# Regrouped sums, early first steps of two layers, and a moved verdict in a four-layer graph network

## The chip, the core and the metric

The kernel runs on one core of one Trainium2 chip. The metric is the device time of one execution in microseconds, as the median of several runs. A core has a matrix engine (TensorE, PE in the profile; PEld is its loading of weights), VectorE (DVE), ScalarE (ACT), GpSimd (POOL) and SyncE (SP), which here only issues DMAs. Each engine takes its instructions in order. DMAs are issued by SP, ACT or POOL, and stand in that engine's queue like any other instruction.

## The reference

A graph network of four layers on x, 2708 nodes of 512 float32 features, with a dense 0/1 adjacency matrix adj (2708 x 2708, int32, symmetric, some 2.3% ones). Every layer normalizes, cuts at zero, and adds its result to x:

```python
h = jnp.maximum(_layernorm(x, axis=-1), 0.0)
x = x + layer(h, adj)
```

The layers, cut to what matters:

```python
# layer 0
out = (a.T @ X) @ weight
out = relu(out * norm[:, None])            # norm = clip(in_degree, 1) ** -0.5
# layer 1: only the first 64 neighbours of a row count
keep = Ab & (jnp.cumsum(Ab, axis=1) <= 64)
xj = leaky_relu((keep @ X / cnt) @ W_nb.T + b_nb)
xi = leaky_relu(X @ W_line.T + b_line)
out = xi + xj
# layer 2: graph attention, 8 heads of 64
Wh = einsum('nd,hdo->hno', x, W)           # f1, f2 = Wh . a1, Wh . a2
e = leaky_relu(f1[:, :, None] + f2[:, None, :], 0.2)
attention = softmax(where(adj > 0, e, NEG_INF))
out = elu(attention @ Wh)
# layer 3
self_f = x @ W_self + b_self
nb_f = (mask @ x / deg) @ W_nb + b_nb
out = relu(concat([self_f, nb_f]) @ W_comb + b_comb)
```

## The kernel before

**Tiling.** The nodes lie in NC = 22 chunks of R = 126 rows; the last chunk has 62. Helper `move` (lines 88 to 99) is one DMA for a full chunk (line 99) and two for the last, 48 and 14 rows (lines 96, 97). A layer first has a dense part, with its product by the weights, and then sums over neighbours. A float32 product is kept as two parts (`halves`), so that a sum costs two matmuls per pair of chunks, one for the last chunk, whose two parts share a tile. PSUM has eight buffers (`ps`), each holding one accumulator, product or set of transposes.

**Sums.** The 22 chunks of results are worked in groups of 4, 4, 4, 4, 3, 3 (line 102): for each group the loop runs over all 22 chunks m, so that a unit (group, m) makes one weight tile of up to 504 columns from the stored pattern vT, and multiplies it with the halves of chunk m into the group's accumulators. For layers 1 and 3 this is `aggregate` (lines 339 to 367). The weight tile is made two units ahead in three buffers; at m = 11 `before` issues the loads for the group's results; the accumulators of a group are taken over by `after` in the first units of the next group, one chunk per unit, and those of the last group after the last unit. For layer 1 the weight tile is a comparison and product on VectorE (`weight1`, L594), and `after1` makes two VectorE operations (L607, L610), an add on GpSimd (L613) and a store. For layer 3 it is a cast on VectorE (`weight3`, L1161), and `after3` is two VectorE operations (L1170, L1173) and a store of the output on ACT's queue.

**Layer 0's sums** have a list of their own with staged delays (lines 399 to 528): adjacency block loaded (`load0`), counted (`count0`), its sign taken (`sign0`), multiplied (`multiply0`), which also transposes the pattern into vT. At the end of a group, `multiply0` scales by the degree, with relu on ACT (L505) or VectorE (L496) by turns, and adds to x on GpSimd (L508).

**Dense parts.** `dense` gives four stages, `load`, `normalize` (`norm`: statistics L188, L190, a square root on ACT L192, then hn at L200 or L202), `transpose` (`relu_T`, four transposes L211 and a relu to hT L213) and `multiply`. `staged` runs stage k of chunk c at step c + k. x tiles have five buffers; hn, y and the output share three buffers by their tag "t". Further stages are appended to the list: for layer 1 `save_last` and `spread_last`; for layer 2 `save_last2`, `sums2` (dot products f1 and f2, L783, L785) at lag 4 and `rows2` at lag 5, which turns a chunk's f1 into a row (`row2`, L796) and starts, in its last four chunks, the attention's first steps (`make`, L724).

**Start and end.** In the preamble (lines 272 to 312) each of two weights is turned (16 transposes at L287, four copies on ACT L288), then multiplied by W_comb (`fused`, L293). In the end a verdict is worked out ahead of layer 3's sums (lines 1133 to 1157): short reductions over the degrees, f12 and the largest weights say whether the fast way holds; a matmul sums them over partitions (L1150). All engines read it behind the kernel, to decide whether a general way has to run, which doesn't happen with this input.

Kernel time therefore runs: preamble, layer 0's dense part and sums, layer 1's dense part and sums, layer 2's dense part, attention, layer 3's dense part, layer 3's sums. The order of the instructions on each engine is that of the program, apart from small movements by the scheduler.

Of the kernel before, what the change touches and what calls it, by code (L numbers as in the profile page):

```python
# [44 lines left out]
def fast_layers(  # L45
# [58 lines left out]
    groups = [list(range(sum(sizes[:g]), sum(sizes[: g + 1]))) for g in range(len(sizes))]  # L104
    KMAX = max(sizes)
# [110 lines left out]
    def staged(count, *stages):  # L216

        for step in range(count + max(lag for lag, _ in stages)):
            for lag, fn in stages:
                if 0 <= step - lag < count:  # L220
                    fn(step - lag)
# [50 lines left out]
    with tc.tile_pool(name="pre", bufs=2) as pre:  # L272
# [9 lines left out]
        for i in range(2):  # L282
            wsT = pre.tile([P, NF, D], F32, name="wsT")
            for f in range(NF):
                pt = ps.tile([P, NF, P], F32, name="wsT_ps", tag="ps")
                for k in range(NF):
                    nc.tensor.transpose(pt[:, k, :], ws[i][:, f, k * P : (k + 1) * P], ident)  # L287
                nc.scalar.copy(wsT[:, :, f * P : (f + 1) * P], pt)  # L288
            wf = pre.tile([P, NF, D], F32, name="wf")
            for f in range(NF):  # L290
                po = ps.tile([P, D], F32, name="fused_ps", tag="ps")
                for k in range(NF):
                    nc.tensor.matmul(  # L293
                        po,
                        wsT[:, k, f * P : (f + 1) * P],
                        wc[:, i * NF + k, :],
                        start=(k == 0),
                        stop=(k == NF - 1),
                    )
                nc.vector.tensor_copy(wf[:, f, :], po)  # L300
            nc.gpsimd.dma_start(fused[i].rearrange("(k p) o -> p k o", p=P), wf)
# [37 lines left out]
    def aggregate(weight_of, parts, before, after, lead=2):  # L339

        units = [(g, m) for g in range(len(groups)) for m in range(NC)]
        weight, loaded, acc = {}, {}, {}

        def make(i):
            g, m = units[i]
            weight[i] = weight_of(m, groups[g])

        def multiply(i):  # L350
            g, m = units[i]
            cs = groups[g]
            if m == 0:
                for c in cs:
                    acc[c] = ps.tile([P, D], F32, name="acc", tag="ps")
            for k, c in enumerate(cs):
                matmuls(acc[c], parts[m], weight[i], k, m)
            del weight[i]
            if m == NC // 2:
                loaded.update((c, before(c)) for c in cs)  # L360
            if g and m < len(groups[g - 1]):
                c = groups[g - 1][m]
                after(c, acc.pop(c), loaded.pop(c))

        staged(len(units), (0, make), (lead, multiply))
        for c in groups[-1]:
            after(c, acc.pop(c), loaded.pop(c))
# [7 lines left out]
    with ExitStack() as ring_ctx:  # L375
        ring = ring_ctx.enter_context(tc.tile_pool(name="ring", bufs=NC - 1, side="right"))

# [16 lines left out]
        with tc.tile_pool(name="l0", bufs=2) as wk:  # L394
# [59 lines left out]
            def multiply0(i):  # L454
# [29 lines left out]
                nc.scalar.copy(vT[g][:, :, m * R : (m + 1) * R], pt[:R, :K, :R])  # L484
                if m == NC // 2:
                    xs.update((c, load_x(x_in, c)) for c in cs)
# [4 lines left out]
                for k, c in enumerate(cs):  # L491
                    n = rows(c)
                    xc = xs.pop(c)
                    r = common.tile([P, D], F32, name="y", tag="t", bufs=3)
                    if k % 2:
                        nc.vector.tensor_scalar(  # L496
                            r[:n],
                            acc.pop(c)[:n],
                            0.0,
                            nrm[:n, k : k + 1],  # L500
                            op0=ALU.max,
                            op1=ALU.mult,
                        )
                    else:
                        nc.scalar.activation(  # L505
                            r[:n], acc.pop(c)[:n], AF.Relu, scale=nrm[:n, k : k + 1]
                        )
                    nc.gpsimd.tensor_tensor(xc[:n], xc[:n], r[:n], ALU.add)  # L508
                    sums1[c] = xc
# [76 lines left out]
        staged(NC, *dense(x1, product1), (3, save_last), (4, spread_last))  # L586
# [17 lines left out]
        def after1(c, acc, xc):  # L604
# [8 lines left out]
            nc.gpsimd.tensor_tensor(xc[:n], xc[:n], y[:n], ALU.add)  # L613
            sums1[c] = xc
            if c not in groups[-1]:
                save2(c)
# [12 lines left out]
        aggregate(weight1, h1, before1, after1)  # L629
# [176 lines left out]
    LATE = NC - 4  # L806

    def rows2(c):
# [5 lines left out]
        if c == NC - 4:  # L814
# [4 lines left out]
        if c > NC - 4:  # L819
# [3 lines left out]
    def save_last2(c):  # L823
        if c < len(groups[-1]):
            save2(groups[-1][c])

    more = [(3, save_last2), (4, sums2), (5, rows2)]
    staged(NC, *dense(x2, product2, False, more, scalar=True))
# [252 lines left out]
    with ExitStack() as stack:  # L1081
# [49 lines left out]


        bad = const.tile([P, 7], F32, name="bad")
        with tc.issue_after(final):
            nc.vector.tensor_reduce(bad[:, 0:1], ind, AX.X, ALU.add)
        nc.vector.tensor_reduce(bad[:, 1:2], deg, AX.X, ALU.add)
        nc.vector.tensor_tensor(bad[:, 0:1], bad[:, 0:1], bad[:, 1:2], ALU.subtract)
        nc.vector.tensor_reduce(bad[:, 2:3], deg, AX.X, ALU.min)
        nc.vector.tensor_scalar(bad[:, 2:3], bad[:, 2:3], 0.5, None, op0=ALU.is_lt)
        for i, (op, over, sign) in enumerate(((ALU.max, ALU.is_gt, 1), (ALU.min, ALU.is_lt, -1))):  # L1140
            f = bad[:, 3 + i : 4 + i]
            with tc.issue_after(final):
                nc.vector.tensor_reduce(f, f12.rearrange("p c h -> p (c h)"), AX.X, op)
            nc.vector.tensor_scalar(f, f, sign * F_MAX, None, op0=over)
            nc.vector.tensor_scalar(
                bad[:, 5 + i : 6 + i], wmax[:, i : i + 1], sign * W_MAX, None, op0=over
            )
        nc.vector.tensor_reduce(bad[:, 1:2], bad[:, 2:], AX.X, ALU.max)
        pv = ps.tile([P, 2], F32, name="verdict_ps", tag="ps")
        nc.tensor.matmul(pv[:1], ones, bad[:, 0:2], start=True, stop=True)  # L1150

        differ = small.tile([1, 2], F32, name="differ")
        nc.vector.tensor_scalar(
            differ[:, 0:1], pv[:1, 0:1], float(N - P * NC), None, op0=ALU.not_equal
        )
        nc.vector.tensor_copy(differ[:, 1:2], pv[:1, 1:2])
        nc.vector.tensor_tensor(verdict, differ[:, 0:1], differ[:, 1:2], ALU.add)

# [4 lines left out]

        def before3(c):
            return load_x(x3, c), load_x(s3, c, name="sc", pool=wk, bufs=4)

        def after3(c, acc, loaded):
# [8 lines left out]
            move(nc.scalar, out[c * R : c * R + n, :], xc[:n])  # L1176
# [630 lines left out]
```

## Time and profile before

| | us |
|---|---|
| median of 3 runs | 1862.52 (1861.09 to 1865.51) |
| profiled execution | 1866.35 |
| its span, first to last instruction | 1864.5 |
| mean granted TensorE clock | 0.991 of full speed |

Times within the profile are counted from the span's start. The span in 40 equal slices, each digit the busy share of a slice in tenths, shows how the stages follow:

```profile
PE   8999999989999999989999999999999899999997
PEld 4555776654446887744444344444344455478886
DVE  4655888875444566577889999999999777533333
ACT  2545887862120000046597766776743566400000
POOL 0000111121110112056200000000000222100000
PEclk9999999999999999999999999999999999999999
```

A slice is 46.6 us. Layer 0's sums end at 405 us, layer 1's dense part and sums follow and end at 795.7 (the first of its weight tiles are made far ahead, at 431.1), layer 2's dense part runs to about 900, attention to 1450, layer 3's dense part to 1633 and its sums to 1855. The weight tiles of layers 1 and 3 in the list of groups (busy us, mean ns of one, idle of the engine before them):

```profile
L594 DVE SCALAR_TENSOR_TENSOR kt<-lastr,index,vT 126x504 fp32r<-126x504 int16 (+1 forms) x132 | 105.0, 804 | 82.8 <-PE acc L331 82.8
L1161 DVE CAST kt<-vT 126x504 fp32r<-126x504 int8 (+1 forms) x132 | 52.8, 400 | 141.6 <-PE acc L331 141.5
```

There are 6 groups times 22 units, 132, in both layers. The accumulating matmul is line 331; one takes 0.2325 us when nothing disturbs it.

### The profile page before, as it was taken

To read this page: it belongs to the slowest core of one execution; us is meant where nothing else is said; L and a number is where in the kernel's file an instruction comes from. 1 tells how busy PE (TensorE), PEld (TensorE's weight loads), DVE (VectorE), ACT (ScalarE), POOL (GpSimd) and SP (SyncE) were. 2 spreads that over 40 slices of the span, in tenths; PEclk is the share of its full clock that TensorE was granted. 3 is DMA by queue.
4 is the path that set the end of the run, shared out by engine and by line. 5 is a ranking of instruction groups with operands and counts; after the bars stand their busy time and mean duration, and the time that the engine had idled before them with its cause. 6 is when DMAs were issued, how large, how long until landed. Compare 5 with 4: busy or idle time off the path is not lost.

```text
span 1864.5 us, 30673 instructions
## 1 busy us (share of the span) xinstructions
PE 1808.8 (97%) x11878; PEld 1053.9 (57%) x11878; DVE 1315.9 (71%) x1949; ACT 843.1 (45%) x1536; POOL 214.6 (12%) x194
## 2 busy tenths in 40 slices
PE   8999999989999999989999999999999899999997
PEld 4555776654446887744444344444344455478886
DVE  4655888875444566577889999999999777533333
ACT  2545887862120000046597766776743566400000
POOL 0000111121110112056200000000000222100000
PEclk9999999999999999999999999999999999999999
DMA  6423555542223112243321220221112444303221
GB/s 209 136 79 95 159 156 155 148 127 63 71 73 82 45 45 68 63 142 106 104 73 37 58 54 15 58 60 40 28 33 51 119 134 136 100 22 106 93 67 44
DMA packets 126039, 161.03 MB, mean 86 GB/s; under 512 B 57406, under 2 KB 77994, under 8 KB 125002
## 3 DMA queue, kind: packets, MB, share of 16 engines
q1 hardware_dynamic: 106764, 123.51, 23.1%
q10 hardware_dynamic: 18544, 33.37, 5.5%
q0 software_dynamic: 576, 2.10, 0.4%
q8 instruction: 95, 1.56, 0.3%
q14 instruction: 60, 0.49, 0.1%
HBM read 111.34 MB, written 47.42 MB: 85 GB/s over the span
## 4 chain that ended last, share of the span: by engine, by line
PE 62%; DVE 16%; issue 5%; DMA 4%; ACT 2%; POOL 1%; DVEq 0%; SPq 0%; ACTq 0%; POOLq 0%
PE acc L331 27%; DVE t L724 10%; PE av L908 8%; PE nb_ps L183 8%; PE line_ps L183 4%; PE sums L908 4%; PE self_ps L183 4%; PE wh_ps L183 3%; DVE cum L429 3%; DMA rb<-rT 2%; PE hT_ps L211 1%; DMA x<-x 1%; DMA ai<-in_adj 1%; PE vT_ps L472 1%; ACT cum L444 1%
## 5 line engine op out<-in xcount | busy, mean ns | idle before, releaser
L724 DVE SCALAR_TENSOR_TENSOR t<-rb,ec,vT 126x2708 f32<-126x2708 f32 (+2 forms) x220 | 532.4, 2470 | 16.7 <-PE sums L908 9.8
L908 PE MATMUL av<-t,whs 126*32 126x451 f32 (+3 forms) x4576 | 434.7, 513 | 0.6 <-DVE ln_mv L190 0.6
L331 PE MATMUL acc<-halves,kt 126*126 126x512 f32 x1848 | 431.1, 394 | 0.5 <-DVE kt L594 0.5
L331 PEld LDWEIGHTS acc<-halves,kt 126*126 126x126 f32 x1848 | 343.7, 186 | 85.5 <-DVE kt L594 1.9
L908 PEld LDWEIGHTS av<-t,whs 126*32 126x32 f32 (+1 forms) x4576 | 161.7, 110 | 203.8 <-issue 179.8
L331 PE MATMUL acc<-halves,ar 126*126 126x512 f32 x924 | 254.7, 415 | 5.2 <-ACT vT L484 4.6
L742 ACT ACTIVATE b<-t,eb 126x2708 bf16<-126x2708 f32 (+1 forms) x78 | 199.0, 2551 | 22.1 <-DVE t L724 22.0
L331 PEld LDWEIGHTS acc<-halves,ar 126*126 126x126 f32 x924 | 164.7, 188 | 49.9 <-issue 9.2
L594 DVE SCALAR_TENSOR_TENSOR kt<-lastr,index,vT 126x504 fp32r<-126x504 int16 (+1 forms) x132 | 105.0, 804 | 82.8 <-PE acc L331 82.8
L1161 DVE CAST kt<-vT 126x504 fp32r<-126x504 int8 (+1 forms) x132 | 52.8, 400 | 141.6 <-PE acc L331 141.5
L429 DVE TENSOR_TENSOR_SCAN cum<-ai,deg 126x504 int16<-126x504 int32 (+2 forms) x110 | 126.1, 1157 | 34.5 <-DMA ai<-in_adj 20.3
L192 ACT ACTIVATE ln_rs<-ln_mv,eps 126x1 f32<-126x1 f32 x88 | 25.4, 293 | 276.5 <-DVE ln_mv L190 270.4
L908 PE MATMUL sums<-t,whs 126*32 126x338 f32 (+5 forms) x1568 | 139.1, 448 | 6.0 <-ACT out L947 5.8
L713 ACT ACTIVATE whs<-wh,ef 126x64 f32<-126x64 f32 x220 | 76.3, 349 | 126.6 <-PE sums L908 72.8
L875 POOL TENSOR_SCALAR z<-y 126x512 f32<-126x512 f32 x22 | 44.0, 2000 | 662.5 <-DVE y L868 653.8
L444 ACT ACTIVATE cum<-cum,limit 126x504 int16<-126x504 int16 (+3 forms) x132 | 88.4, 670 | 64.3 <-DVE deg L437 62.3
L188 DVE BATCH_NORM_STATS2 ln_st<-x 126x6 f32<-126x512 f32 x88 | 60.4, 687 | 56.5 <-DMA x<-x 46.4
L908 PEld LDWEIGHTS sums<-t,whs 126*32 126x32 f32 (+1 forms) x1568 | 55.3, 109 | 73.6 <-issue 37.7
L183 PE MATMUL nb_ps<-wfn,hT 128*126 128x512 f32 x176 | 80.9, 603 | 3.1 <-ACT hT L213 3.1
L183 PE MATMUL wh_ps<-w2s,hT 128*126 128x512 f32 (+1 forms) x176 | 82.8, 615 | 0.0
L484 ACT CAST vT<-vT_ps 126x504 int8<-126x504 f32 (+1 forms) x132 | 69.9, 535 | 26.6 <-DVE sums L475 17.1
L183 PE MATMUL h_ps<-w0s,hT 128*126 128x512 f32 x176 | 80.1, 598 | 1.3 <-ACT hT L213 1.3
(174 smaller groups left out, 1981.8 us busy)
## 6 DMA issues: line engine op xcount, KB each, us to landing
x<-x SPq DMA_DIRECT2D x105, 252.0 KB
x<-x ACTq DMA_DIRECT2D x84, 252.0 KB
ai<-in_adj SPq DMA_DIRECT2D x84, 249.0 KB
x<-in_x SPq DMA_DIRECT2D x42, 252.0 KB
rb<-rT SPq DMA_DIRECT2D x7, 1332.8 KB
wh<-whd SPq DMA_DIRECT2D x70, 94.5 KB
whd<-wh SPq DMA_DIRECT2D x21, 252.0 KB
aT<-avT SPq DMA_DIRECT2D x21, 252.0 KB
```

The costliest lines, as they stand in the source:

```text
L183: nc.tensor.matmul(po[:n], lhsT[:, f, :n], w[:, f, :], start=(f == 0), stop=(f == NF - 1))
L188: nc.vector.bn_stats(st[:n], xc[:n])
L331: nc.tensor.matmul(acc[:R], weight[:, k * R : (k + 1) * R], parts[:, i, :], start=(m == 0 and i == 0), stop=(m == NC - 1),)
L429: nc.vector.tensor_tensor_scan(cum[:n, :gw], ai[:n, :gw], ai[:n, :gw], 0.0 if g == 0 else deg[:n, m : m + 1], op0=ALU.add, op1=ALU.max,)
L444: nc.scalar.activation(cum[:n, :gw], cum[:n, :gw], AF.Sign, bias=limit[:n], scale=-1.0, accum_out=signs[:n, m, g : g + 1],)
L484: nc.scalar.copy(vT[g][:, :, m * R : (m + 1) * R], pt[:R, :K, :R])
L594: nc.vector.scalar_tensor_tensor(by_chunk(kt, cs), lastr[:, cs[0] * R : (cs[-1] + 1) * R].rearrange("p (c r) -> p c r", r=R), index[:R, m ...
L713: nc.scalar.activation(t[:q, :O], wh.pop((u, m))[:q], AF.Copy, scale=by)
L724: ins = nc.vector.scalar_tensor_tensor(t[:q, : hi - lo], row[h][:q, lo:hi], ec[:q, m, h : h + 1], vT[g][:q, k, lo:hi], op0=ALU.max, op1=AL ...
L742: nc.scalar.activation(b[:q, : hi - lo], weight[s][:q, : hi - lo], AF.Sigmoid, bias=eb[:q, m, h : h + 1], scale=STEEP,)
L908: nc.tensor.matmul(p[j * S : (j + 1) * S, : b - a], lhsT, rhs[:, part * size + a : part * size + b], start=(s % NC == 0), stop=(s % NC == ...
L1161: nc.vector.tensor_copy(by_chunk(kt, cs), pattern(m, cs))
```

## The change

It has seven parts.

1. In the preamble both weights get their tiles at the front. The second weight's transposes and copies are put between the first weight's product rows 1 and 2.
2. `aggregate` (layers 1 and 3) uses `spans` of 4, 4, 4, 4, 3, 2, 1 chunks; layer 0's sums and the pattern keep the groups. A seventh span adds 22 units and 22 weight tiles to each of the two layers; there are as many matmuls as before.
3. The first three steps of the dense part of layer 1 are issued at m = 9, 13 and 18 of layer 0's last group, those of layer 2 at the same places of layer 1's last span; `staged` goes on from step 3 (`done`).
4. In layer 0's last group the relu stays in PSUM, and the add to x runs on VectorE. In layer 1's last span the add runs on VectorE too.
5. `rows2` comes one step later (lag 6), and the attention's first steps begin at chunk NC - 5 in place of NC - 4, so at the same step as before.
6. The verdict is a function `judge`, called from `before3` in the middle of layer 3's third span.
7. The last chunk's output goes out as 16 rows on ACT's queue and 46 on SP's, in place of 48 and 14 on ACT's.

```diff
+    cuts = [0, 4, 8, 12, 16, 19, 21, NC]
+    spans = [list(range(a, b)) for a, b in zip(cuts, cuts[1:])]
...
-    def staged(count, *stages):
+    def staged(count, *stages, done=0):
-        for step in range(count + max(lag for lag, _ in stages)):
-            for lag, fn in stages:
-                if 0 <= step - lag < count:
-                    fn(step - lag)
+        for step in range(done, count + max(lag for lag, _ in stages)):
+            emit_step(step, count, stages)
+
+    def emit_step(step, count, stages):
+        for lag, fn in stages:
+            if 0 <= step - lag < count:
+                fn(step - lag)
...
+        turn_weight(0)
+        for f in range(NF):
+            if f == NF // 2:
+                turn_weight(1)
+            fuse(0, f)
+        for f in range(NF):
+            fuse(1, f)
...
-    def aggregate(weight_of, parts, before, after, lead=2):
+    def aggregate(weight_of, parts, before, after, lead=2, ahead=()):
...
-        units = [(g, m) for g in range(len(groups)) for m in range(NC)]
+        units = [(g, m) for g in range(len(spans)) for m in range(NC)]
...
             if m == NC // 2:
                 loaded.update((c, before(c)) for c in cs)
+            if g == len(spans) - 1:
+                for at_m, fn, *args in ahead:
+                    if m == at_m:
+                        fn(*args)
...
+        AHEAD = (9, 13, 18)
+        stages1 = dense(
+            x1,
+            lambda *args: product1(*args),
+            more=[(3, lambda c: save_last(c)), (4, lambda c: spread_last(c))],
+        )
...
+                if g == len(groups) - 1 and m in AHEAD:
+                    emit_step(AHEAD.index(m), NC, stages1)
...
+                    po = acc.pop(c)
+
+                    r = po
+                    if g < len(groups) - 1:
+                        r = common.tile([P, D], F32, name="y", tag="t", bufs=3)
...
-                    nc.gpsimd.tensor_tensor(xc[:n], xc[:n], r[:n], ALU.add)
+                    eng = nc.gpsimd if g < len(groups) - 1 else nc.vector
+                    eng.tensor_tensor(xc[:n], xc[:n], r[:n], ALU.add)
...
-        staged(NC, *dense(x1, product1), (3, save_last), (4, spread_last))
+        staged(NC, *stages1, done=len(AHEAD))
...
-            nc.gpsimd.tensor_tensor(xc[:n], xc[:n], y[:n], ALU.add)
+            eng = nc.vector if c in spans[-1] else nc.gpsimd
+            eng.tensor_tensor(xc[:n], xc[:n], y[:n], ALU.add)
             sums1[c] = xc
-            if c not in groups[-1]:
+            if c not in spans[-1]:
                 save2(c)
...
+        stages2 = dense(
+            x2,
+            lambda *args: product2(*args),
+            False,
+            [(3, lambda c: save_last2(c)), (4, lambda c: sums2(c)), (6, lambda c: rows2(c))],
+            scalar=True,
+        )
+        ahead = [(m, emit_step, step, NC, stages2) for step, m in enumerate(AHEAD)]
+        aggregate(weight1, h1, before1, after1, ahead=ahead)
...
-    LATE = NC - 4
+    LATE = NC - 5
...
-        if c == NC - 4:
+        if c == LATE:
...
-        if c > NC - 4:
+        if LATE < c <= LATE + 3:
...
+        def judge():
...
         def before3(c):
+            if c == 2 * KMAX:
+                with tc.issue_after(final):
+                    judge()
...
-            move(nc.scalar, out[c * R : c * R + n, :], xc[:n])
+            half = n // 32 * 16 if c == NC - 1 else n
+            nc.scalar.dma_start(out[c * R : c * R + half, :], xc[:half])
+            if half < n:
+                nc.sync.dma_start(out[c * R + half : c * R + n, :], xc[half:n])
```

The body of `judge` is the verdict of before, word for word, but for the `issue_after` marks, which now stand around the call. The bodies of `turn_weight` and `fuse` are the two inner loops of the preamble, and the DMA of a fused weight is issued behind its fourth row.

## The prediction

> **What bounds the kernel now.** I read the engine totals first, then the list of what the matrix engine waited for, then the timeline and the granted clock around each of those waits. The totals:
>
> ```profile
> PE 1808.8 (97%) x11878; PEld 1053.9 (57%) x11878; DVE 1315.9 (71%) x1949; ACT 843.1 (45%) x1536; POOL 214.6 (12%) x194
> ```
>
> TensorE (PE) is busy for 1808.8 of 1864.5 us, so all but 55.7 us of the span is matrix work, and the change leaves the number of matmuls as it is. It can only win inside those 55.7 us, and in the stretches where PE runs at a lowered clock behind a gap. Who causes the gaps (engine, line waited for, us in total, times, longest):
>
> ```profile
> PE hT_ps L211 <- DVE hn L202: 6.4, 3, 4.2
> ...
> PE hT_ps L211 <- ACT hn L200: 5.3, 2, 4.3
> ...
> PE fused_ps L293 <- ACT wsT L288: 3.2, 2, 2.5
> ...
> PE f_ps L796 <- DVE f L785: 3.0, 2, 2.7
> PE verdict_ps L1150 <- DVE bad L1148: 2.7, 1, 2.7
> ```
>
> Each of these five is touched by the change. The PE timeline shows where they lie, and what follows a gap (start, length, then in brackets the idle time before):
>
> ```profile
> 409.49 1.07 PE L211 MATMUL hT_ps<-ident,hn 126*128 126x126 f32 x4 [4.20 <-DVE hn L202]
> 410.90 1.07 PE L211 MATMUL hT_ps<-ident,hn 126*128 126x126 f32 x4 [0.33 <-DVE hn L202]
> 411.77 5.16 PE L183 MATMUL nb_ps<-wn,hT 128*126 128x512 f32 x8
> 416.76 3.60 PE L183 MATMUL line_ps<-wl,hT 128*126 128x512 f32 x8
> ```
>
> Four transposes cost 0.6 us and eight products 3.60 at full clock. After the gap they take 1.07 and 5.16: the granted clock was 0.51 from 408 to 412 and 0.64 from 412 to 416. A gap thus costs its idle time and a slow stretch behind it.
>
> **The change part by part.** Sums are made against the profiled execution, 1866.35 us (span 1864.5); the median of the runs, 1862.52, lies 3.8 below it, and I take the same gain off that.
>
> *1. Preamble.* PE waits 2.50 at 28.38 because the four copies of the second turned weight (27.77 to 29.79 on ACT) stand behind a table load and square roots from 24.43 on. In the new order these transposes and copies come between the second and third of the first weight's four product rows, at about 16, before that table load. The second weight's loads were issued from 8.13 to 10.47, so they have landed. The first weight's last two product rows (3.9 us each, 15.7 for four) cover the copies (4 x 0.5). Gain **2.5** (0 if the copies still fall behind the roots).
>
> *2. Layer 0 to layer 1.* The last sum ends at 405.3; before, PE next transposes the third normalized chunk at 420.19. After, the first chunk's transposes lie among the last sums; the second chunk's run at 405.5, its neighbour follows: products 406.1 to 409.5 and 409.5 to 413.0. Then the third chunk is late. Its x1 load needs the buffer of chunk 19, whose way out still begins at the same place: two relus of 0.62 from 405.82, an add (now VectorE's instead of GpSimd's), the second chunk's transposed relu (0.59) ahead of the store on ACT's queue, store issued near 407.9. On SP the load stands behind bl, bn and the copies of vT, whose issues end at 407.89, so they hold nothing up. From the old rows: store to load issue 407.88 to 411.32, load to statistics 413.91. Statistics of the next chunk sit before hn on VectorE (0.7), then reciprocal and hn (0.7): transposes at 416.0, a gap of 3.0 us. What the gap does to the clock decides 1.7 us. The Trainium skill's page "TensorE: Matmul & The Clock Gate", in its section on the HAM clock gate, says that the clock falls after a whole idle window of about 3.4 us and that only gaps above this are to be avoided; by it the clock stays. The nearest row is layer 2's:
>
> ```profile
> 875.80 0.37 PE L796 MATMUL f_ps<-ident,f 126*8 126x126 f32 x1 [2.71 <-DVE f L785]
> 875.96 1.05 PE L211 MATMUL hT_ps<-ident,hn 126*128 126x126 f32 x4
> 876.80 4.75 PE L183 MATMUL wh_ps<-w2s,hT 128*126 128x512 f32 x8
> ...
> 876.00:880.00 4.00, 4.00 (x10) 2.19 (x9) 4.00 (x5) 3.43 (x6) 1.80 (x1) 0.61 0.03 5
> ```
>
> After 2.71 us of idling, four transposes took 1.05 and eight products 4.75; the last line is the window from 876 to 880, whose third number from the end is the clock, 0.61. So the row contradicts the threshold and I let the clock fall: 416.0 + 1.7 = 417.7 against 420.19, gain **2.5**; by the rule 4.1. Ends: -1 (the round trip of 5.3 us from store issue to hn gets 2 to 3 us longer because more DMAs are under way) and +5 (no gap).
>
> *3. Layer 1 to layer 2.* Before, from 764.89 the last group of three chunks takes 30.0 us of sums (129 matmuls of 0.2325), then idle 0.48, 4.26 and 1.03, a clock of 0.57 from 800 to 808, and the third chunk's transposes at 808.40: 43.5 us in all. After, the same sums come as a group of two and a group of one, with two chunks' transposes (0.86) and one's products (3.44) among or right behind them: 34.3. That is 9.2 less, minus stalls of the narrow groups. A weight tile of three chunks costs VectorE 0.61 (row of 126x378); four cost 0.85 in the mean. At some 1.04 ns per column over a fixed 0.2, two chunks cost 0.47 and one 0.3, while PE needs 0.93 and 0.465 per unit (four and two matmuls of 0.2325). So VectorE keeps up alone, but not with what else it gets: per finished chunk 0.74 + 0.68 for y, four statistics at 0.69 in the one-chunk group, and GpSimd's adds, beside which the 126x378 rows of 0.61 became 0.99, 1.25 and 0.90. In 22 units of 0.465 (10.2 us) VectorE would owe 22 x 0.3 + 2 x 1.42 + 4 x 0.9 = 13.0, against 10.2 + 3.4 us of the products that lie behind unit 19; three tiles in store, and waits for statistics' loads (the stores that free their buffers stand behind hn of the first two chunks on ACT's queue), make me take 2 us of stall there, and 2 for the two-chunk group that takes over three chunks. Gain 9.2 - 4.0 = **5.2** (3 to 8).
>
> *4. Layer 2's rows.* f (L785) waited on VectorE behind attention's first products t (1.66 each), and PE behind f: 2.71 at 875.80, 1.6 of slow clock after it, 0.66 at two earlier places. With the row turned one step (3.97 us) later, f is done at 875.65, and PE would want it at 877: gain **4.7** (2 to 5; f still late by a part of a step). The exponentials and makes stay at the same steps; one more row falls to the last steps, 0.37 us of PE and one store, beside attention's work.
>
> *5. Verdict.* PE waits 2.72 at 1634.85, because its verdict matmul needs the reductions on VectorE. In the new order the matmul lies in the third group. The first weight cast (0.41) follows the last y at 1632.85 and one or two reductions: PE starts at 1633.4 instead of 1634.97, gain **1.5** (1 to 2). The eleven short operations lie between casts of 0.41, of which PE needs one per 1.86 us. That register loads of the verdict queue behind sixteen more loads on SP costs nothing: nothing reads it before the end.
>
> *6. Layer 3's narrow groups.* Casts are 0.42 (504 columns) and 0.36 (378), so 0.25 for one chunk, under PE's 0.465. In the last group, the two finished chunks add 4 x 0.7 among six casts that PE would use up in 2.8 us: 2.8 + 1.5 of VectorE work against 2.8 and three tiles in store. Loss **1.3** (0 to 2); the two-chunk group none.
>
> *7. Tail.* PE ends at 1854.81, then six VectorE operations run to 1858.36 and the last store issues at 1859.08. With one chunk left it is two operations (0.74 + 0.68): 1856.3, and both stores issue then, on two queues. That is 2.8 earlier. But the last store is cut 16 + 46 rows instead of 48 + 14. The page "DMA: Bandwidth & Descriptors", section "Why a DMA increments its semaphore by 16 and not by 1", says a transfer is spread over the largest number of engines up to 16 that divides its slowest dimension: 46 rows get 2 engines, 23 rows of 2 KB each. The row is the scalar queue's total,
>
> ```profile
> q10 hardware_dynamic: 18544, 33.37, 5.5%
> ```
>
> 18544 packets in 5.5% of sixteen engines' span, 88 ns each: 23 in a row are 2.0 us, where the 14 rows that ended the kernel took one packet on each of 14 engines, 0.1. By the packet row alone (spread evenly) the gain is 2.8, by the rule 0.9, and no row here shows such a transfer. I take **0.9**, since the packet's time is measured and only the count rests on the page.
>
> Sum: 2.5 + 2.5 + 5.2 + 4.7 + 1.5 - 1.3 + 0.9 = **16.0**. The profiled execution would be 1850.3, the median **1846.5**.
>
> **The rivals.** *The round trips fill the gaps again* (0.20): in parts 2 and 3 the third chunk needs store, load and statistics of a buffer just freed. If each such trip takes 5 to 6 us in place of the 5.3 counted up to hn, plus waits for statistics in the narrow group, parts 2 and 3 give nothing: 16.0 - 7.7 = 8.3, 1854.2. For it: the DMA engines were 0.74 and 0.66 busy in the windows 408 to 412 and 804 to 808, when such trips were under way. Against it: the first chunks' trips now lie among sums. *All is hidden* (0.12): clock kept, no stalls, 46 rows as quick as 48: 16 + 1.6 + 3 + 1.9 = 22.5, 1840.0. *One-chunk units outrun VectorE* (slower, 0.04): the 44 one-chunk units have 0.465 us of PE work and three weight tiles; a tile is built after PE lets one go. If that loop takes over 2.6 us for three tiles, each unit costs 0.41 more and 18 us are eaten: 1864.5. It decides from 0.87 us per unit on. For it: the longest weight tile took 1.78 beside GpSimd. Against it: VectorE stands idle for 82.8 us before layer 1's weight tiles and 141.5 before layer 3's casts. *The scheduler leaves the order as it was* (0.02): 1862.5; the order of PE's instructions in the changed program speaks against it. The remaining 0.62 is the forecast, with 1843 to 1851 as its own range.
>
> **How the numbers follow.** The range reaches from 1838.5 (just below all-hidden) to 1855.5 (round trips back), leaving the slower rival and extremes out. A difference of 0.2%, 3.7 us, is what can be told from none. Faster: 0.62 + 0.12 + 0.19 = 0.93; same 0.03 (order kept, and the worst of the round trips); slower 0.04.
>
> **What would show it.** In the changed profile: no wait for wsT at the start; a transposition right behind the last sum near 405 and again near 790, with one gap of about 3 us behind the second chunk's products in layer 1; no wait for f; no wait for the verdict; weight-tile waits of some 4 us in layer 1's and 1.3 in layer 3's last groups; the last store's packets on two engines. Wrong it would be if the one-chunk groups show PE waits at every unit, or if the third chunk's transposes wait over 5 us for hn.

## The result, and the profile after

The changed kernel took 1851.55 us in the median of four runs (1846.91 to 1852.72), beside 1863.88 for the kernel before on the same chip: a ratio of 0.9931, 95% interval 0.9909 to 0.9953. Run again with six executions on another chip it took 1851.18 beside 1864.61, ratio 0.9924 (0.9909 to 0.9938). The profiled execution took 1852.72, with a span of 1850.8. All lines of the changed kernel's code have moved: transposes are L214 (before L211), dense products L186 (L183), hn L205 (L202), the sums' matmul L348 (L331), weight tiles L623 and L1170 (L594 and L1161), layer 0's cast of the adjacency block L450.

Engine totals of the changed kernel:

```profile
PE 1805.7 (98%) x11878; PEld 1050.0 (57%) x11878; DVE 1323.8 (72%) x1997; ACT 843.7 (46%) x1536; POOL 211.8 (11%) x190
```

The span is 13.6 us shorter. PE is idle for 1850.8 - 1805.7 = 45.1 us instead of 55.7, which is 10.6, and its busy time fell by 3.1 with the same 11878 matmuls. Less of it runs at half clock: apart from the program's start and end, the stretches at half clock come to 17.1 us instead of 27.3. What PE waits for now (us in total, times, longest):

```profile
PE hT_ps L214 <- DVE hn L205: 6.2, 2, 4.4
...
PE acc L348 <- DVE ar L450: 2.6, 3, 1.9
...
PE acc L348 <- DVE kt L623: 2.1, 4, 1.0
...
PE acc L348 <- DVE kt L1170: 1.4, 1, 1.4
...
PE av L945 <- ACT whs L751: 0.8, 1, 0.8
```

The waits for the turned weight, for f and for the verdict are gone, and so is that for layer 2's hn on ACT (5.3 before). The wait for hn from VectorE is as large as before (6.2 for 6.4). Four are new or larger: layer 0's adjacency tile (0.3 before), layer 1's weight tiles (0.5 before), whs in the attention, and the first weight tile of layer 3 (L1170), whose 1.4 us stand where the verdict's 2.7 stood.

To see where the time went I took the start of the same matmul in both traces at nine places, and the end of the span as a tenth. The table has what the changed kernel had gained since the place before it, in us, for both of its profiles:

| up to | predicted | first profile | second profile |
|---|---|---|---|
| bias product, end of the preamble | 2.5 | 6.7 | 6.0 |
| last matmul of layer 0's sums | 0 | -2.2 | -1.6 |
| layer 1, fourth chunk | 2.5 | 0.5 | 1.2 |
| layer 2, third chunk | 5.2 | 5.2 | 5.2 |
| first matmul of the attention | 4.7 | 5.2 | 5.1 |
| its 800th av matmul | 0 | -2.6 | -1.6 |
| layer 3, third chunk | 0 | -1.8 | -3.8 |
| first matmul of layer 3's sums | 1.5 | 1.5 | 1.5 |
| last matmul | -1.3 | -1.1 | -1.1 |
| end of the span | 0.9 | 2.3 | 2.4 |
| sum | 16.0 | 13.6 | 13.4 |

The largest miss in one place is the step to layer 1. PE there, in the changed kernel (start, length, in brackets the idle time before):

```profile
400.66 0.59 PE L214 MATMUL hT_ps<-ident,hn 126*128 126x126 f32 x4
401.09 3.60 PE L186 MATMUL nb_ps<-wn,hT 128*126 128x512 f32 x8
404.53 3.60 PE L186 MATMUL line_ps<-wl,hT 128*126 128x512 f32 x8
412.50 1.07 PE L214 MATMUL hT_ps<-ident,hn 126*128 126x126 f32 x4 [4.38 <-DVE hn L205]
413.37 5.87 PE L186 MATMUL nb_ps<-wn,hT 128*126 128x512 f32 x8
```

The first gap of 4.20 is gone: products start right behind the second chunk's transposes. But a gap of 4.38 stands where the third chunk is due, one set of products later, and the slow clock has come along with it (5.87 for eight products of 3.60). The gap has moved from the first chunk to the third.

### The profile page after: what moved, and what is told of

Its sections match the earlier page's. It is cut to its first block, busy times and chain, and to the rows that moved or that the text cites. A ratio compares the mean times of both kernels' runs of the same rounds, so it can differ in the third digit from the quotient of the medians.

```text
span 1850.8 us, 30734 instructions
## 1 busy us (share of the span) xinstructions
PE 1805.7 (98%) x11878; PEld 1050.0 (57%) x11878; DVE 1323.8 (72%) x1997; ACT 843.7 (46%) x1536; POOL 211.8 (11%) x190
## 4 chain that ended last, share of the span: by engine, by line
PE 61%; DVE 16%; issue 5%; DMA 4%; ACT 2%; POOL 0%; SPq 0%; DVEq 0%; ACTq 0%; POOLq 0%
PE acc L348 25%; PE av L945 10%; DVE t L762 9%; PE nb_ps L186 8%; PE sums L945 4%; PE wh_ps L186 4%; PE self_ps L186 4%; PE line_ps L186 4%; DVE cum L458 4%; DMA rb<-rT 2%; PE hT_ps L214 1%; DMA ai<-in_adj 1%; DMA x<-x 1%; DVE ar L450 1%; ACT cum L473 1%
## 5 line engine op out<-in xcount | busy, mean ns | idle before, releaser
L762 DVE SCALAR_TENSOR_TENSOR t<-rb,ec,vT 126x2708 f32<-126x2708 f32 (+2 forms) x220 | 532.6, 2471 | 21.5 <-PE sums L945 12.4
L348 PE MATMUL acc<-halves,kt 126*126 126x512 f32 x1848 | 434.8, 395 | 3.7 <-DVE kt L623 2.1
L348 PEld LDWEIGHTS acc<-halves,kt 126*126 126x126 f32 x1848 | 342.6, 186 | 92.5 <-DVE kt L623 6.2
L348 PE MATMUL acc<-halves,ar 126*126 126x512 f32 x924 | 253.2, 413 | 6.5 <-ACT vT L513 3.5
L348 PEld LDWEIGHTS acc<-halves,ar 126*126 126x126 f32 x924 | 163.8, 187 | 51.0 <-issue 9.2
L623 DVE SCALAR_TENSOR_TENSOR kt<-lastr,index,vT 126x504 fp32r<-126x504 int16 (+3 forms) x154 | 110.4, 728 | 81.7 <-PE acc L348 81.5
L1170 DVE CAST kt<-vT 126x504 fp32r<-126x504 int8 (+3 forms) x154 | 56.0, 366 | 137.8 <-PE acc L348 137.8
L186 PE MATMUL nb_ps<-wfn,hT 128*126 128x512 f32 x176 | 81.2, 605 | 2.0 <-ACT hT L216 2.0
L186 PE MATMUL nb_ps<-wn,hT 128*126 128x512 f32 x176 | 81.4, 606 | 0.0
L186 PE MATMUL h_ps<-w0s,hT 128*126 128x512 f32 x176 | 79.9, 597 | 1.4 <-ACT hT L216 1.1
```

The source lines that it names most:

```text
L186: nc.tensor.matmul(po[:n], lhsT[:, f, :n], w[:, f, :], start=(f == 0), stop=(f == NF - 1))
L348: nc.tensor.matmul(acc[:R], weight[:, k * R : (k + 1) * R], parts[:, i, :], start=(m == 0 and i == 0), stop=(m == NC - 1),)
L623: nc.vector.scalar_tensor_tensor(by_chunk(kt, cs), lastr[:, cs[0] * R : (cs[-1] + 1) * R].rearrange("p (c r) -> p c r", r=R), index[:R, m ...
L762: ins = nc.vector.scalar_tensor_tensor(t[:q, : hi - lo], row[h][:q, lo:hi], ec[:q, m, h : h + 1], vT[g][:q, k, lo:hi], op0=ALU.max, op1=AL ...
L1170: nc.vector.tensor_copy(by_chunk(kt, cs), pattern(m, cs))
```

## The experiments

In all, twelve runs in three sessions. The kernel before took 1864.61, 1865.99 and 1867.18 in them, so kernels of different sessions are compared by their ratios to it, and places by their traces. The changed kernel itself came first, as the base of the others.

> The changed kernel once more, beside the runs of before on the same chip. Theory 'places' (each gap that the change shortens pays its own idle time and the half-clock stretch behind it): ratio to before 0.993 +- 0.001, about 12.5 us less, and the same stage gains as in the first profile: 4.7 us by the end of layer 0's sums, 0.4 at the step to layer 1's dense part, 5.2 at the step to layer 2, 5.2 in layer 2's dense part, 2.5 given back at the start of the attention. Rival 'clock luck' (half-clock stretches that fall here or there by chance make most of it): two or more of these stages differ by over 1.7 us from the first profile, and the ratio by over 0.003.

Measured: ratio 0.9924. The second profile is in the table above. The gains at the ten places repeat within 0.75 us but for two, the attention's start (1.0 apart) and the stretch behind it (2.0 apart). So most of the gain sits firmly in its places, and it differs most in the stretch from the attention to layer 3, in which no instruction was changed. What differs there is said in the last section.

**Which wait keeps layer 1's gap open.** The x of chunk 19 goes into a buffer that the last group leaves free:

```diff
-def load_x(src, c, name="x", pool=None, bufs=XBUFS, twice=False):
+def load_x(src, c, name="x", pool=None, bufs=XBUFS, twice=False, tag=None):
...
-xs.update((c, load_x(x_in, c)) for c in cs)
+xs.update(
+    (c, load_x(x_in, c, tag="t", bufs=3) if c == groups[-1][0] else load_x(x_in, c))
+    for c in cs
+)
```

> The x of chunk 19 is loaded into one of the three buffers that y and hn share, which the last group of layer 0 leaves free, so that the third chunk's x1 has a buffer of its own and is loaded and normalized among the last sums. Theory 'buffer' (the gap of 4.38 us at 412.50 and the slow clock behind it come from the third chunk's x1 waiting for chunk 19's store): the third chunk's transposes follow the first chunk's products without a gap and at full clock, 6 to 7.5 us less than the changed kernel. Rival 'queue' (the chain of loads behind the stores is late for any chunk): the wait moves to the fourth chunk, and at most 2 us are won.

Measured: 1844.22, ratio 0.9894 (0.9877 to 0.9911), 7.0 us less than the changed kernel of the same session, whose interval (0.9909 to 0.9938) its own just overlaps. The same place on PE, in this kernel:

```profile
398.77 0.59 PE L214 MATMUL hT_ps<-ident,hn 126*128 126x126 f32 x4
399.20 3.60 PE L186 MATMUL nb_ps<-wn,hT 128*126 128x512 f32 x8
402.64 3.60 PE L186 MATMUL line_ps<-wl,hT 128*126 128x512 f32 x8
406.07 0.59 PE L214 MATMUL hT_ps<-ident,hn 126*128 126x126 f32 x4
406.50 3.60 PE L186 MATMUL nb_ps<-wn,hT 128*126 128x512 f32 x8
```

The third chunk's transposes begin when the first chunk's products end, and everything runs at 0.59 and 3.60. The step to layer 1 gains 7.76 instead of 0.5 to 1.2. One missing buffer was the whole gap: five x tiles held chunks 19, 20 and 21 and the first two of layer 1, and the sixth had to wait for a store, a load and its statistics.

**Whether the early steps or the adds closed the first gap.** Layer 1's early steps taken out (`if False` in place of the test for AHEAD, and `staged(NC, *stages1)`), the rest kept:

> The changed kernel with layer 1's first three steps put behind layer 0's sums again. Theory 'buffer': they are worth little without a free buffer for the third chunk, because its wait takes over: third chunk's transposes 0.4 to 1.5 us later against the end of the sums, total the same within 1.5. Rival, the step of the prediction: 2.5 us slower.

> The kernel without layer 1's early steps once more, since it came out 6 us faster than the changed kernel, though its profiled execution was only 1.3 us faster. Theory 'threshold' (its gap before the third chunk's transposes is 3.4 us in place of 4.4, so that the half clock behind it comes in some executions and not in others): its times spread over 8 us or more, median 1843 to 1850, and if the profiled execution has no half clock near 411 its third chunk's products run at 3.6 us at once. Rival 'chance' (the few times were a lucky draw): median within 2 us of the changed kernel, 0.9924 +- 0.001 of before.

Measured in two sessions: ratio 0.9878 (0.9842 to 0.9914) and 0.9888 (0.9868 to 0.9908). Without the early steps the kernel is no slower: by its ratios it is 0.0046 and 0.0036 faster than the changed kernel, where only the second pair of intervals doesn't touch. Its ten times spread over 10 us (1841.54 to 1851.55), as the "threshold" theory has it. That theory isn't shown, though: both profiled executions were among the slower ones (1851.55 and 1849.33), they gained only 1.1 and 3.3 us on the changed kernel's first profile, and in both the clock fell. The gap before the third chunk is shorter in them, 3.44 and 3.63, here in the second:

```profile
413.26 0.62 PE L214 MATMUL hT_ps<-ident,hn 126*128 126x126 f32 x4 [3.63 <-DVE hn L205]
413.72 5.29 PE L186 MATMUL nb_ps<-wn,hT 128*126 128x512 f32 x8
```

By the ratios this kernel is also as fast as the one with chunk 19's buffer (0.9894), although its gap is still there in both profiles. Since only slower executions were profiled, which wait makes its fast ones fast isn't shown.

And the early steps have a price that I had not seen. VectorE and PE in the changed kernel, in the middle of layer 0:

```profile
341.26 0.69 DVE L191 BATCH_NORM_STATS2 ln_st<-x 126x6 f32<-126x512 f32 x1 [3.20 <-DMA x<-x]
341.87 0.99 DVE L458 TENSOR_TENSOR_SCAN cum<-ai,deg 126x378 int16<-126x378 int32 x1
...
343.37 1.65 PE L348 MATMUL acc<-halves,ar 126*126 126x512 f32 x6 [1.94 <-DVE ar L450]
```

The statistics of layer 1's first chunk have been put far ahead, wait 3.20 us there for their load, and hold up the scans and casts behind them on VectorE; PE runs dry for 1.94. A gap of 1.8 to 3.4 us lies between 339 and 346 in all ten profiles of kernels with these early steps, and in none of the four without (the kernel before, these two, and the last one below).

The other way round, the relus in shared buffers and the adds on GpSimd as before, with the early steps kept:

> The changed kernel with layer 0's last relus in the shared buffers and its last adds on GpSimd again, the early steps of layer 1 kept. Theory 'adds' (the adds on VectorE closed the first gap, and on GpSimd they make the stores, and with them the third chunk's load, later): the gap before the third chunk's transposes grows from 4.4 by 1 to 2.5 us, 1 to 3 us slower than the changed kernel. Rival 'steps' (the early steps closed it alone): within 0.7 us.

Measured: 1851.52, ratio 0.9915 (0.9897 to 0.9932), so the same as the changed kernel; the gap before the third chunk was 4.31, no longer than before. "Adds" falls. Either of the two edits alone removes the gap of 4.20 before the first chunk's transposes; without the early steps 1.25 us of waiting remain between the transposes and the first product.

**What is lost at the attention's start.** SP issues in the changed kernel:

```profile
892.14 0.36 SPq L738 DMA_DIRECT2D wh<-whd  x1
895.58 0.33 SPq L719 DMA_DIRECT2D rb<-rT  x1
899.13 0.31 SPq L738 DMA_DIRECT2D wh<-whd  x1
899.49 0.45 SPq L719 DMA_DIRECT2D rb<-rT  x1
```

The kernel before issued both row loads (rb) at once, 12.4 us behind the attention's first matmul:

```profile
909.53 0.84 SPq L681 DMA_DIRECT2D rb<-rT  x2
```

Now the second one is issued 17.8 us behind it, because a load of wh stands between them, and that one waits for a buffer. The exponential of that row then starts at 908.14, and the scaled weights behind it on ACT come late:

```profile
910.89 1.37 PE L945 MATMUL av<-t,whs 126*32 126x346 f32 x16 [0.76 <-ACT whs L751]
```

The edit that turns two rows at the first step: `behind(max(1, c - LATE), row2, c)` in place of `behind(c - LATE + 1, row2, c)`.

> The five last rows of f are turned at attention's steps 1, 1, 2, 3, 4 in place of 1 to 5. Theory 'row' (the row of head 1 is loaded some 5 us late because the fifth row's store comes one step later and a load of wh then stands in front of it on SP): the two row loads are issued one behind the other, the waits for whs near 910 go, and 2.2 to 2.6 us less than the changed kernel. Rival 'order' (the loss of 2.5 us at attention's start has another reason on PE or comes with the clock): the time stays within 0.7 us.

Measured in its trace: both row loads in one go,

```profile
894.54 0.77 SPq L719 DMA_DIRECT2D rb<-rT  x2
899.54 0.32 SPq L738 DMA_DIRECT2D wh<-whd  x1
```

no wait for whs, and a loss of 0.1 us up to the 800th matmul in place of 2.6 and 1.6. Two further kernels with this edit also lose 0.1. In the time it doesn't show: 1850.65, ratio 0.9930 (0.9915 to 0.9946) beside 0.9924. In this profile, 6.8 us of half clock at 1033 took the place of 3.4. In all eight other profiles of kernels with the new rows and without this edit the second row is late too, but only two of the nine, the changed kernel's first and one without layer 1's early steps, show a wait for whs, and these lose 2.6 and 2.5 us; the others lose 0.4 to 1.6. So the mean loss is smaller than I took it to be from the first profile.

The other half of part 5, undone: lag 5 and NC - 4 again.

> The changed kernel with the rows of f one step earlier and four of them in the attention's steps, as before the change. Theory 'places': the wait for f of 2.7 us with its half-clock stretch returns (5.2 us by the attention's start), the loss of 2.5 us at attention's start goes, 2.7 us slower in all. Rival: the f gap alone, 5 us slower; or no difference, if the gap shrinks since the third chunk of layer 2 is no longer late.

Measured: 1855.88, ratio 0.9938 (0.9920 to 0.9956), which is 0.0014 or 2.6 us above the changed kernel, with overlapping intervals: the time alone doesn't tell them apart. Its trace has the old wait again,

```profile
866.22 0.27 PE L834 MATMUL f_ps<-ident,f 126*8 126x126 f32 x1 [2.71 <-DVE f L823]
866.33 0.94 PE L214 MATMUL hT_ps<-ident,hn 126*128 126x126 f32 x4
867.05 4.98 PE L186 MATMUL wh_ps<-w2s,hT 128*126 128x512 f32 x8
```

and gains 0.95 in layer 2's dense part where the changed kernel gains 5.2, but loses nothing (0.00) at the attention's start. By the traces part 5 is worth 4.3 and pays some of it back at once.

**The preamble's order**, undone:

> The changed kernel with the preamble's old order (the second weight turned behind the first one's products). Theory 'places': PE waits some 2.5 us near 28 and runs some 3.4 us at half clock behind it, the bias product comes 5.5 to 6.7 us later than in the changed kernel, and of that 4.5 to 5 are left at the end of layer 0's sums and in the total. Rival 'absorbed': layer 0's sums wait for their adjacency blocks anyway, which move with the DMAs and not with PE, so that their end and the total move by 2 us at most.

Measured: 1853.66, ratio 0.9938 (0.9921 to 0.9956), 2.6 us above the changed kernel by the ratios, with overlapping intervals. PE waits again,

```profile
23.95 1.91 PE L295 MATMUL wsT_ps<-ident,ws 128*128 128x128 f32 x16
27.91 14.00 PE L301 MATMUL fused_ps<-wc,wsT 128*128 128x512 f32 x32 [2.04 <-ACT wsT L296]
```

this time without a slow stretch: 32 matmuls in 14.00, where the kernel before needed 15.70 at a clock of 0.65 and 0.93:

```profile
28.38 15.70 PE L293 MATMUL fused_ps<-wc,wsT 128*128 128x512 f32 x32 [2.50 <-ACT wsT L288]
```

The bias product comes 4.5 us later than in the changed kernel's first profile, and at the end of layer 0's sums 2.7 of that are left. Both theories held a half: layer 0 absorbs part, not most.

Not all of these 4.5 us are the gap's, though. Every profile begins with PE at half speed, here in the changed kernel, where the same 16 transposes take 4.04 us at first and 1.91 later:

```profile
3.75 4.04 PE L295 MATMUL wsT_ps<-ident,ws 128*128 128x128 f32 x16 [3.75 <-DMA ws<-in_L_gnn_W_self]
14.85 1.91 PE L295 MATMUL wsT_ps<-ident,ws 128*128 128x128 f32 x16
```

Products of the preamble start 0.85 us apart up to some moment, and 0.43 us apart from then on. The moment is that of the first clock record in the trace. It came at 8.3 and 9.9 us in the changed kernel's two profiles, at 7.1 to 12.1 in all twelve profiles with the new order of the preamble, at 12.1 in the kernel before and at 12.4 in this one. A microsecond later costs half a microsecond. With that taken off, the bias product starts at 33.0 to 33.7 in all twelve, at 35.7 here and at 38.0 in the kernel before. So the gap is worth 2.5, a gap with a slow stretch behind it 4.8, and the other 1.9 of the first profile's 6.7 come from the start. Whether the new order brings full speed on earlier or that is chance, the runs don't show: its latest case is as late as the kernel before.

**The narrow groups and layer 2's early steps.** First the early steps of layer 2 taken out, the narrow groups kept (`ahead = []`, `staged(NC, *stages2)`), then the other way round (`cuts = [0, 4, 8, 12, 16, 19, NC]`):

> The changed kernel with layer 2's first three steps put behind layer 1's sums again, the narrow groups kept. Theory 'steps' (the early steps fill the gap, the narrow groups alone don't): a gap of 3 us or more before the first transposes and slow clock behind it, 4 to 7 us slower. Rival 'groups' (one chunk left over at the end is what shortens the wait): at most 1.5 us slower.

> The changed kernel with the old groups 4, 4, 4, 4, 3, 3 in layers 1 and 3, the early steps kept in the last group of three. Theory 'steps': the step to layer 2 keeps its gain within 2 us, layer 3's sums win 1.1, the end loses 2.3: the total within 2.5 us. Rival 'groups': without the narrow last group the third chunk's transposes wait for buffers of the last three chunks, with a gap of 4 us or more, and the total is 4 us slower or more.

Measured: without the early steps 1854.13, ratio 0.9925 (0.9895 to 0.9956); with the old groups 1854.15, ratio 0.9935 (0.9913 to 0.9956). By the times neither can be told from the changed kernel. The traces say more, as gains over the kernel before:

| | changed (two profiles) | no early steps | old groups |
|---|---|---|---|
| step to layer 2 and its dense part | 10.4, 10.3 | 7.1 | 9.4 |
| layer 3's sums | -1.1, -1.1 | -1.1 | -0.3 |
| end | 2.3, 2.4 | 2.5 | -0.1 |

So layer 2's early steps are worth 3.2 in these traces, of which 1.7 are one stretch of half clock (787.8 to 791.2) in the profile without them. The gap that I expected without them wasn't there (0.34 before the first transposes): the narrow group alone removes most of it. The early steps alone remove it too, but with the old groups a gap of 1.97 comes up before layer 2's fifth chunk (806.81). The narrow groups are worth some 0.9 in layer 1 and 2.4 at the end, and cost 0.8 in layer 3's sums: about 2.5 in all.

**Together.** Chunk 19's buffer, two rows at the first step, and the last output as 48 and 14 rows on two queues:

> Both edits, and the last chunk's output in 48 rows on ACT's queue and 14 on SP's. Theory 'places': the gains add up, 6.5 + 2.4 + 1.2 = 10.1 us less than the changed kernel, about 1841. Rival: a gain in front only makes a later transfer the wait, 1846 or more.

Measured: 1844.53, ratio 0.9889 (0.9871 to 0.9907), a gain 3.5 us smaller than was expected. The step to layer 1 gains 7.76 and the attention's start loses 0.1, as they should, but this profile lost 5.0 in layer 0 (a gap of 3.37 at the early statistics, with half clock behind it). And the split of the output gave nothing: the last data of the output landed 3.85 us behind PE's end instead of 4.67, but the span ended 7.61 behind it instead of 7.38.

Last, the same without that split and without layer 1's early steps:

> Chunk 19's x in a shared buffer, two rows of f at the attention's first step, and no early steps of layer 1 written out. Theory 'places': no gap between layer 0 and layer 1, no wait for whs at attention's start, and no extra work among layer 0's last sums: 1 to 3 us less than the kernel with chunk 19's x in a shared buffer alone, 1840 to 1843. Rival: the early steps were needed for the third chunk, which waits 2 us or more again: 1845 or more.

Measured: 1844.14 (1842.12 to 1845.47), ratio 0.9871 (0.9852 to 0.9890). It has no gap before layer 1 and none near 341, and it is the lowest ratio of all. It lies in the intervals of the two kernels with chunk 19's buffer above, and in those of the kernel that only leaves the early steps out (0.9878 and 0.9888): by the times the four can't be told apart. Against the changed kernel (0.9924, 0.9909 to 0.9938) the intervals don't touch: some 0.5% was left, 7 us by the medians and 10 by the ratios.

## Why the prediction was right, and where not

The sum came out near, 16.0 against 13.6 in the profile and 12.3 to 13.4 in the medians. The medians of 1851.2 and 1851.6 lie in the stated range, but just past the 1843 to 1851 that the forecast gave as its own. That it came so near is in part luck: misses of both signs stood beside each other.

- *Preamble, 2.5.* The term was too small, by the slow stretch behind the gap: I counted 2.50 of idle time and not the windows of clock 0.65 and 0.93 behind it (1.7 us), though I priced just this in two other places. Another 1.9 of the 6.7 came from the half speed at the program's start, which ended earlier; no term of the sum looked at it. On the other side I left out that layer 0 takes part of it back. At the end of layer 0's sums 4.5 stood, and undoing the part alone cost 2.6 us by the ratios, not clear of the noise.
- *Layer 0 to layer 1, 2.5.* Here the step failed. The wait that I named (store, load, statistics of the third chunk, from chunk 19's buffer) is the right one, and removing it was worth some 7 us, at this place and in the medians. But the gap was 4.38 for 3.0 and the slow stretch cost 2.7 for 1.7. From store to load it took 4.14 us where I took 3.44 from the old row; and from the third chunk's statistics to its transposes it took 3.14 where I had counted 2.1. On VectorE the next chunk's statistics stood in front of the third chunk's reciprocal and waited 0.74 for their own load. I had put these statistics into the sum at their 0.7 us of work, without their wait. So the edit that the sum credits gained 0.5 to 1.2 here; the early steps even cost a gap in the middle of layer 0 that I did not look for, since I priced what they take from the end and not what an early instruction holds up where it is put.
- *Layer 1 to layer 2, 5.2.* Right, in its parts too: 5.2. From the start of the two-chunk group to the third chunk's transposes (759.87 to 798.23) it took 38.4 us for the 34.3 of sums, transposes and product, so 4.1 of stall where I took 4.0. The list of waits shows only 2.1 of them, since many are too short for it. A one-chunk weight tile took 0.33 to 0.35 us (estimate 0.3), one of two chunks 0.48 (estimate 0.47).
- *Layer 2's rows, 4.7.* 5.2 came, and the f wait is gone. That "one more row falls to the last steps", at 0.37 us of PE, is the other step that failed: the row cost a place in SP's queue, where a load of wh came between the two row loads, and 0.4 to 2.6 us were lost. I had looked for slack up to the row's use, not for what passes it in the queue.
- *Verdict 1.5 and layer 3's narrow groups -1.3.* 1.5 and -1.1, in both profiles. The 1.1 are short stalls of the last group (1833.5 to 1835.8 us), where I had put them.
- *Tail, 0.9.* 2.3 came, near the 2.8 of the row. The rule on the spreading of a DMA (the page "DMA: Bandwidth & Descriptors") was right: in the trace's packet records of the 46 rows, packets of 2 KB and 84 ns come in pairs, in two chains, the last at 1848.1, where the queue with 16 rows had ended at 1846.7. But nothing waited for them: with 48 and 14 rows the data landed 0.8 sooner and the end came no sooner. I took a measured transfer time for a part of the path without a row that showed the end waiting for it. In both traces loads of instructions (queue q14) go on until 0.7 us or less before the span's end; whether the end waits for these isn't shown.
- *The rivals.* "The round trips fill the gaps again" was half true, for layer 1's step alone. "One-chunk units outrun VectorE" didn't happen: the stall of both narrow groups of layer 1 is 4.1 us, not 18.
- *The clock.* At the one place where I weighed the threshold of the Trainium skill's page "TensorE: Matmul & The Clock Gate" (section on the HAM clock gate) against the row, the gap came out above the threshold, so that place doesn't decide it. Other gaps of these traces do, and against it: 11 of the 18 between 3.03 and 3.27 us had half clock at them.

## What to carry to other kernels

When a gap at a change of stage is closed, ask which buffer the next tile in line needs, and count the buffers that are held at that moment: here the reorderings only moved the gap, and one more free buffer closed it (7.76 us at this place for 0.5 to 1.2). In the time, leaving the early steps out gained as much as the buffer did, so a part that only moves a gap can be left out. An instruction that is put early on an engine working in order holds up all that stands behind it until its load has landed, so place the load early and the operation on it late. And price a step that moves a DMA by the DMAs that can pass it in its queue, not by its own duration.

## What the runs showed of the hardware

The traces' records of the granted clock begin 7.1 to 12.4 us into the span; the preamble's products before that start 0.85 us apart instead of 0.43, so at half speed. From there on the clock is full but for stretches at one half, each of 3.41 or 6.83 us, apart from one in each profile that lies behind the last sums and reaches to the program's end. Over the 14 profiles of this case, all 13 gaps on PE of 3.37 us or more behind the start had such a stretch in them or within 2 us behind them; of the 18 gaps between 3.03 and 3.27 us, 11 had one; of the five between 2.35 and 2.72, four. The gap of 1.83 us at the step to layer 3, always the same, was followed by one in 10 of the 14 profiles. So below 3.4 us the length of the gap alone doesn't decide it here. A stretch costs up to half its length, 1.7 or 3.4 us. Between the 800th av matmul and layer 3's third chunk the changed kernel's two profiles have three and four windows of 3.41 us, where the profile of before has one, and that bears the loss of 1.8 and 3.8 us there. So the times of one kernel spread with the number of stretches that it happens to get. What decides a single case the runs don't show.
